# A tile of its own for the unread output of the x3 sums, and four rows of factors in one tile instead of eight in two

## The chip, the cores and the metric

One core of a Trainium2 chip runs the whole program. The time is the device time of one execution in microseconds (us), as the median of three runs. The core has TensorE (PE; PEld are its weight loads), VectorE (DVE), ScalarE (ACT), GpSimd (POOL) and SyncE (SP), which here issues nearly all DMA transfers.

## The reference, cut to what matters

`x` is a field of 256 x 256 tokens with 128 channels. Four layers are added to it one after the other; each reads a group normalisation of `x`. The change lies in the third, which makes x3 out of x2:

```python
zn = _layernorm(z, ln_in_w, ln_in_b)          # z = _gn(x2)
a = sigmoid(zn @ Wga + bga) * (zn @ Wla + bla)
b = sigmoid(zn @ Wgb + bgb) * (zn @ Wlb + blb)
k = jnp.einsum('bimc,bmjc->bijc', a, b)
out = sigmoid(zn @ Wgo + bgo) * (_layernorm(k, ln_o_w, ln_o_b) @ Wlo + blo)
x3 = x2 + out
```

The fourth layer begins with a group normalisation of x3, so the sums of x3 and of its square over all tokens are needed before it can start.

## The kernel before, in words

The channels lie on the 128 partitions, the 65,536 tokens along the free dimension, cut into 32 superchunks of 2048 (`SC`); all data is fp32. The layer has three stages. The first makes `a` and `b` and stores for each token the layer norm's factor, one row of 2048 numbers for each superchunk (`rs2D`). The second, the product stage (L1260 to L1298), multiplies `a` by `b` channel by channel and stores `k`. The third, the x3 stage (from L1305), makes x3 out of x2, `k` and the factors. Within these stages the order of the instructions on each engine is the order in which they are written (`manual_schedule`). Waits follow from the tiles: who writes a tile waits for those who still read or write it.

An iteration `s` of the x3 stage's loop does the following, in two halves `h` of 1024 tokens where a half is named:

- SP: load the row of factors of superchunk s+6 (`load_row7`, L1249), load `k` of s+3 (L1314, four tiles).
- `gate7(s + 3, h)`: TensorE multiplies x2 by the gate's weights (L1334); VectorE adds a column and multiplies by the spread factors into the gate tile (L1344); ScalarE takes the sigmoid in place (L1345). The gate tiles `p7_g` are five, so gate s+5 goes into the tile of gate s. Gates 0 to 2 are made in a prologue ahead of the loop, with the first four spread rows. The gates of superchunks 30 and 31 were made two stages before; iterations 27 to 31 therefore make none.
- TensorE multiplies the normalised `k` of s by the output weights (L1334 again); VectorE adds the bias and multiplies into the gate tile (L1388).
- In half 0, TensorE spreads the layer norm factors of `k` for s+1 over the partitions (L1087), and GpSimd spreads the row of s+4 (`spread_z`, L1328, two tiles). VectorE multiplies `k` of s+1 by its factors (L1323), in each half.
- After both halves, GpSimd adds the gate tile to x2 (L1401), which makes x3 of s. Then `finish7(s - 1)`: ScalarE takes the sum of x3 (L1348) and of its square (L1349) of the superchunk before, through the accumulator of an ACTIVATE whose elementwise output nobody reads; SP stores x3 (L1354). Last SP loads x2 of s+5 (L1258, seven tiles), which needs the tile of s-2: stored and summed.

Each of the ACTIVATEs in L1348 and L1349 must write its output somewhere. Before the change it is the gate tile of the superchunk (`gts.pop(s)` as `junk`).

The rows of factors lie in two tiles, `rs2_0` and `rs2_1`, on the partitions 0, 32, 64 and 96 of each, eight rows in all (`row7`). Six rows are loaded at the head of the product stage (L1279 to L1280), each further one in the loop.

Of the kernel before, what the change touches and what calls it, by code (L numbers as in the profile page):

```python
# [9 lines left out]
F32 = mybir.dt.float32  # L10
# [6 lines left out]
P = 128  # L17
# [3 lines left out]
SC = 2048  # L21
# [11 lines left out]
def kernel(ctx: ExitStack, tc: tile.TileContext, a: dict, out: bass.AP):  # L33
# [205 lines left out]
    with tc.tile_pool(name="x0", bufs=1) as xres, tc.tile_pool(name="p0", bufs=3) as sb:  # L239
        held = {s: xres.tile([P, SC], F32, name=f"x0_{s}") for s in range(RES, NSC)}  # L240
        with tc.tile_pool(name="p0ps", bufs=3, space=PSUM) as ps, tc.tile_pool(
            name="f0ps", bufs=2, space=PSUM
# [167 lines left out]
        with tc.tile_pool(name="p1", bufs=2) as wk_sb, tc.tile_pool(  # L410
            name="p1ps", bufs=4, space=PSUM
# [70 lines left out]
    with tc.tile_pool(name="p2e", bufs=6) as eb, tc.tile_pool(name="p2c", bufs=1) as cs:  # L482
        triT = cs.tile([P, NH, 2, N], F32, name="triT")
        with tc.tile_pool(name="p2", bufs=2) as sb, tc.tile_pool(
            name="p2S", bufs=2, space=PSUM
        ) as psS, tc.tile_pool(name="p2z", bufs=1, space=PSUM) as psZ, tc.tile_pool(
            name="p2M", bufs=3, space=PSUM
# [361 lines left out]
    with x1_scope:  # L849
        with tc.tile_pool(name="p3", bufs=3) as sb, tc.tile_pool(  # L850
            name="p3ps", bufs=3, space=PSUM
# [41 lines left out]
        with tc.tile_pool(name="z", bufs=2) as sb, tc.tile_pool(  # L893
            name="zps", bufs=3, space=PSUM
# [28 lines left out]
            at = turn_z(0)  # L923
            for k in range(16):
                nxt = turn_z(k + 1)
                pz = tri_multiply(nc, ps, at, AB[k // 2][1], k % 2).rearrange("p t n -> p (t n)")
                at = nxt
# [32 lines left out]
        with tc.tile_pool(name="p4", bufs=3) as sb, tc.tile_pool(  # L960
            name="p4psg", bufs=2, space=PSUM
        ) as psg, tc.tile_pool(name="p4psz", bufs=2, space=PSUM) as psz, tc.manual_schedule():
            zs, gts, sums = {}, {}, []
            junk = sb.tile([P, SC], F32, name="p4_junk", bufs=1)
# [41 lines left out]
            for i, s in enumerate(order):  # L1006
# [14 lines left out]
                for h in range(2):  # L1021
                    hs = slice(h * 2 * CK, (h + 1) * 2 * CK)
# [5 lines left out]
                if i in by_dve:  # L1028
                    for h in range(2):
                        hs = slice(h * 2 * CK, (h + 1) * 2 * CK)  # L1030
# [70 lines left out]
    with tc.tile_pool(name="x5", bufs=7) as x5_pool, tc.tile_pool(name="p5", bufs=2) as sb, tc.tile_pool(  # L1101
        name="p5q", bufs=4
    ) as sq_pool, tc.tile_pool(name="p5psX", bufs=1, space=PSUM) as psX, tc.tile_pool(
        name="p5psM", bufs=3, space=PSUM
# [83 lines left out]
        for h, rb in enumerate(broadcast_rows(psM, var, 0, "p5_pm", tag="p5_pm")):  # L1188
            hs = slice(h * H2, (h + 1) * H2)
# [48 lines left out]
    rk_pool = rs2_scope.enter_context(tc.tile_pool(name="rk", bufs=1))  # L1238
    x7_pool = rs2_scope.enter_context(tc.tile_pool(name="x7", bufs=3))
    rk = rk_pool.tile([P, CK], F32, name="rk")  # L1240
    rs2 = [rk_pool.tile([P, SC], F32, name=f"rs2_{i}") for i in range(2)]

    def row7(s):
        at = 32 * (s % 4)
        return rs2[s // 4 % 2][at : at + 1, :]

    def load_row7(s):
        if s < NSC - 2:
            nc.sync.dma_start(row7(s), rs2D[:, s * SC : (s + 1) * SC])  # L1249
# [10 lines left out]
    with tc.tile_pool(name="p6", bufs=3) as sb, tc.tile_pool(name="p6ps", bufs=3, space=PSUM) as ps:  # L1260
        nc.vector.memset(k1, 0.0)
        nc.gpsimd.memset(k2, 0.0)  # L1262
        with tc.manual_schedule():
            quads = {}

            def load6(q):
                if q < D // 4:
                    A = sb.tile([P, 4, 2 * N], F32, name="p6_A")
                    nc.sync.dma_start(A, aD[:, 4 * q : 4 * q + 4, :])
                    B = sb.tile([P, 4, 2 * N], F32, name="p6_B")  # L1270
                    nc.sync.dma_start(B, bD[:, 4 * q : 4 * q + 4, :])
                    quads[q] = A, B

            def turn6(c):
                return tri_turn(nc, ps, sb, quads[c // 4][0], c % 4, ident, nc.vector.tensor_copy)

            for q in range(3):
                load6(q)
            for s in range(6):  # L1279
                load_row7(s)  # L1280
            at = turn6(0)
            for c in range(D):
                q = c // 4
                if c % 4 == 0:
                    K = sb.tile([P, 4, 2 * N], F32, name="p6_K")
                nxt = turn6(c + 1) if c + 1 < D else None
                pz = tri_multiply(nc, ps, at, quads[q][1], c % 4).rearrange("p t n -> p (t n)")
                at = nxt
                nc.scalar.copy(K[:, c % 4, :], pz)  # L1289
                sq = sb.tile([P, 2 * N], F32, name="p6_sq")  # L1290
                nc.scalar.activation(sq, pz, AF.Square)  # L1291
                nc.vector.tensor_tensor(k1, pz, k1, ALU.add)  # L1292
                nc.gpsimd.tensor_tensor(k2, k2, sq, ALU.add)  # L1293
                if c % 4 == 3:
                    nc.sync.dma_start(kD[4 * q : 4 * q + 4, :].rearrange("c (p t) -> p c t", p=P), K)
                    del quads[q]
                    load6(q + 3)
                    if q >= D // 4 - 3:  # L1298
                        load7x(q - (D // 4 - 3), x7_pool, 3)
# [5 lines left out]
    with tc.tile_pool(name="p7", bufs=2) as sb, tc.tile_pool(name="p7psX", bufs=2, space=PSUM) as psX, tc.tile_pool(  # L1305
        name="p7psM", bufs=2, space=PSUM
    ) as psM, tc.manual_schedule():
        ks, rks, rbs, gts = {}, {}, {}, dict(gates)
        AHEAD = 3

        def load7k(s):
            if s < NSC:
                ks[s] = sb.tile([P, SC], F32, name="p7_k", bufs=4)
                nc.sync.dma_start(ks[s], kD[:, s * SC : (s + 1) * SC])  # L1314

        def spread_k(s):
            if s < NSC:
                rks[s] = broadcast_rows(psX, rk, s, "p7_rk")

        def normalise_k(s, h):  # L1320
            if s < NSC:
                hs = slice(h * H2, (h + 1) * H2)
                nc.vector.tensor_tensor(ks[s][:, hs], rks[s][h], ks[s][:, hs], ALU.mult)  # L1323

        def spread_z(s):
            if s < NSC and s not in gates:
                rbs[s] = sb.tile([P, SC], F32, name="p7_rb")
                nc.gpsimd.partition_broadcast(rbs[s], row7(s))  # L1328

        def product7(src, w, h):  # L1330
            pm = psM.tile([P, 2, CK], F32, name="p7_pm")
            for c in range(2):
                k = 2 * h + c
                nc.tensor.matmul(pm[:, c, :], lhsT=w, rhs=src[:, k * CK : (k + 1) * CK], start=True, stop=True)  # L1334
            return pm.rearrange("p c t -> p (c t)")

        def gate7(s, h):
            if s < NSC and s not in gates:
                hs = slice(h * H2, (h + 1) * H2)
                if h == 0:  # L1340
                    gts[s] = sb.tile([P, SC], F32, name="p7_g", bufs=5)
                pg = product7(xs7[s], wf2[:, 4, :], h)
                zg = gts[s][:, hs]
                nc.vector.scalar_tensor_tensor(zg, pg, gcol, rbs[s][:, hs], ALU.add, ALU.mult)  # L1344
                nc.scalar.activation(zg, zg, AF.Sigmoid, bias=b2w[:, 4:5])  # L1345

        def sums7(x, junk, i):
            nc.scalar.activation(junk, x, AF.Identity, bias=m2neg, accum_out=g1[:, i : i + 1])  # L1348
            nc.scalar.activation(junk, x, AF.Square, bias=m2neg, accum_out=g2[:, i : i + 1])  # L1349

        def finish7(s):
            x = xs7.pop(s)
            sums7(x, gts.pop(s), s)
            nc.sync.dma_start(x3T[:, s * SC : (s + 1) * SC], x)  # L1354

        load7k(0)
        load7x(3, sb, 4)
        spread_z(0)
        spread_z(1)

        nc.vector.scalar_tensor_tensor(k1, k1, -1.0 / D, k1, ALU.mult, ALU.mult)
        nc.vector.tensor_tensor(k2, k2, k1, ALU.add)
        nc.vector.tensor_scalar(k2, k2, 0.0, None, ALU.max)
        nc.scalar.activation(k2, k2, AF.Sqrt, bias=epst, scale=1.0 / D)
        nc.vector.reciprocal(k1, k2)
        nc.sync.dma_start(rkD.rearrange("o (p t) -> p (o t)", p=P), k1)
        for c in range(4):
            nc.sync.dma_start(rk[32 * c : 32 * c + 32, :], rkD.rearrange("o (s c t) -> c (o s) t", c=4, t=CK)[c])
        for s in range(1, 3):
            load7k(s)  # L1370
        load7x(4, sb, 4)
        for s in range(3):
            gate7(s, 0)
            gate7(s, 1)
            if s < 2:
                spread_z(s + 2)
        spread_k(0)
        normalise_k(0, 0)
        normalise_k(0, 1)
        for s in range(NSC):  # L1380
            load_row7(s + 6)
            load7k(s + 3)
            last = s == NSC - 1
            for h in range(2):
                hs = slice(h * H2, (h + 1) * H2)
                gate7(s + AHEAD, h)
                pl = product7(ks[s], w2[:, 5, :], h)
                nc.vector.scalar_tensor_tensor(gts[s][:, hs], pl, b2w[:, 5:6], gts[s][:, hs], ALU.add, ALU.mult)  # L1388
                if h == 0:
                    spread_k(s + 1)  # L1390
                    spread_z(s + AHEAD + 1)
                normalise_k(s + 1, h)
                if last:
                    nc.vector.tensor_tensor(xs7[s][:, hs], xs7[s][:, hs], gts[s][:, hs], ALU.add)
                    if h == 0:
                        finish7(s - 1)
                    sums7(xs7[s][:, hs], gts[s][:, hs], s + h)
                    nc.sync.dma_start(x3T[:, s * SC + h * H2 : s * SC + (h + 1) * H2], xs7[s][:, hs])
            del ks[s]
            if not last:  # L1400
                nc.gpsimd.tensor_tensor(xs7[s], xs7[s], gts[s], ALU.add)  # L1401
                if s:
                    finish7(s - 1)
            load7x(s + 5, *((x7_pool, 3) if (s + 5) % 7 < 3 else (sb, 4)))
# [486 lines left out]
```

## Time and profile before

| | us |
|---|---|
| median of 3 runs | 3400.09 |
| lowest, highest | 3397.42, 3402.27 |
| the profiled execution | 3407.79 |
| its span, first to last instruction | 3405.9 |
| TensorE busy | 3094.3 |
| VectorE, ScalarE, GpSimd busy | 2269.6, 2021.2, 1659.1 |
| x3 stage, about | 2648 to 2970 of the span |

A profile line of a group reads: line, engine, operation, output<-inputs, sizes, count, then busy time and mean duration, then the idle time of the engine just before these instructions and who ended it. A wait reads: the waiting engine and line, "<-", the one whose semaphore came last, us in total, times, longest. A line of the timeline or of the chain begins with the start and the duration in us. Idle time of an engine that isn't the bottleneck costs nothing.

### The profile page before, as it was taken

What the parts mean: (1) busy time and instruction counts of PE and PEld (TensorE: products, weight loads), DVE (VectorE), ACT (ScalarE), POOL (GpSimd) and SP (SyncE); (2) the same over time, 40 slices, a digit from 0 to 9 for tenths busy, and PEclk for the clock granted to TensorE, in tenths of its full rate; (3) what the DMA queues carried; (4) which work ended last, traced back from release to release, by engine and by line L of the source; (5) the groups of instructions that cost most, each with busy time, mean ns of one, the idle gap of its engine ahead of it and who ended that gap; (6) DMA issues with size and microseconds to landing.
All of it is one profiled execution on the core that took longest, in us unless ns stands there. A gap on an engine that the chain in (4) does not pass through costs nothing. (4 is left out here: it accounts for less than half of the span.)

```text
span 3405.9 us, 52131 instructions
## 1 busy us (share of the span) xinstructions
PE 3094.3 (91%) x20036; PEld 1645.1 (48%) x20036; DVE 2269.6 (67%) x2613; ACT 2021.2 (59%) x2209; POOL 1659.1 (49%) x904
## 2 busy tenths in 40 slices
PE   5669999999999999967996999999999888769998
PEld 5415555555555555524332444445998333224444
DVE  5627888888888888853555454454555777657776
ACT  3567777777777777734685444443444566635565
POOL 4055777777777777711582000002555666524444
PEclk7899999999999999989997999999999999879999
DMA  9982333333333333379597677676998888756764
GB/s 359 363 315 85 108 120 110 116 115 112 119 108 120 107 120 107 108 287 337 211 401 303 228 282 301 224 270 252 355 348 334 317 310 307 268 162 192 207 186 131
DMA packets 297908, 749.48 MB, mean 220 GB/s; under 512 B 74551, under 2 KB 145161, under 8 KB 248473
## 3 DMA queue, kind: packets, MB, share of 16 engines
q1 hardware_dynamic: 289719, 735.49, 60.5%
q0 software_dynamic: 7648, 9.55, 0.8%
q8 instruction: 161, 2.64, 0.3%
q10 hardware_dynamic: 288, 1.05, 0.1%
q14 instruction: 92, 0.75, 0.1%
HBM read 458.34 MB, written 287.64 MB: 219 GB/s over the span
## 5 line engine op out<-in xcount | busy, mean ns | idle before, releaser
L565 DVE TENSOR_TENSOR p_e<-p_S,triT 128x1024 f32<-128x1024 f32 x512 | 609.4, 1212 | 144.4 <-PE p_S L555 144.4
L575 POOL TENSOR_TENSOR p_es<-p_e 128x1024 f32<-128x1024 f32 x256 | 603.1, 2367 | 125.7 <-issue 65.1
L573 ACT ACTIVATE p_e<-p_e,mbT 128x1024 f32<-128x1024 f32 x512 | 552.0, 1138 | 61.4 <-DVE p_e L565 61.3
L1172 PE MATMUL p_pm<-p_zn,wf 128*128 128x512 f32 x1040 | 449.3, 593 | 2.5 <-ACT p_a L1207 1.9
L540 PE MATMUL p_mm<-p_xn,w 128*128 128x512 f32 x768 | 405.2, 611 | 0.3 <-DVE p_v L535 0.3
L1172 PEld LDWEIGHTS p_pm<-p_zn,wf 128*128 128x128 f32 x1040 | 196.6, 190 | 255.3 <-issue 246.5
L555 PE MATMUL p_S<-p_q,p_k 32*128 32x256 f32 x4096 | 295.5, 401 | 3.5 <-DVE p_e L565 3.3
L1585 POOL TENSOR_TENSOR p_q<-p_q,p_pb 128x2024 f32<-128x2024 f32 x32 | 144.1, 4502 | 259.5 <-DVE p_pb L1579 247.0
L555 PEld LDWEIGHTS p_S<-p_q,p_k 32*128 32x128 f32 x4096 | 186.0, 184 | 159.5 <-PE p_mm L531 91.7
L514 POOL TENSOR_TENSOR p_xn<-p_xn,p_rs 128x1024 f32<-128x1024 f32 x63 | 151.3, 2401 | 205.3 <-DMA p_rb<-rzD 131.7
L1849 PE MATMUL tp_z<-p_B,tp_at 128*128 128x256 f32 x1024 | 250.4, 388 | 0.8 <-DMA p_B<-bD 0.5
L588 PE MATMUL p_o<-p_e,p_v 128*32 128x256 f32 x4096 | 248.5, 383 | 0.0
L1262 POOL MEMSET k<- 128x512 f32 x1 | 0.5, 519 | 507.0 <-DVE p_zn L1165 507.0
L1293 POOL TENSOR_TENSOR k<-k,p_sq 128x512 f32<-128x512 f32 x128 | 163.0, 1273 | 159.4 <-ACT p_sq L1291 159.4
L1849 PEld LDWEIGHTS tp_z<-p_B,tp_at 128*128 128x128 f32 x1024 | 185.2, 191 | 22.7 <-DVE tp_at L1840 1.6
L1401 POOL TENSOR_TENSOR p_x<-p_x,p_g 128x2048 f32<-128x2048 f32 x30 | 136.0, 4535 | 97.9 <-ACT p_g L1345 59.2
L540 PEld LDWEIGHTS p_mm<-p_xn,w 128*128 128x128 f32 x768 | 126.0, 190 | 104.5 <-issue 88.5
L588 PEld LDWEIGHTS p_o<-p_e,p_v 128*32 128x32 f32 x4096 | 120.2, 110 | 110.3 <-ACT p_g L546 41.5
L1292 DVE TENSOR_TENSOR k<-tp_z,k 128x512 f32<-128x512 f32 x128 | 88.5, 691 | 127.1 <-ACT p_sq L1291 127.1
L1334 PE MATMUL p_pm<-p_x,wf 128*128 128x512 f32 x240 | 121.7, 634 | 53.7 <-DVE p_g L1344 51.8
L1289 ACT COPY p_K<-tp_z 128x512 f32<-128x512 f32 x128 | 74.9, 585 | 157.9 <-PE tp_z L1849 157.9
L546 ACT ACTIVATE p_g<-p_mm,bgh 128x512 f32<-128x512 f32 x128 | 87.9, 687 | 131.4 <-PE p_mm L540 131.3
(380 smaller groups left out, 5957.1 us busy)
## 6 DMA issues: line engine op xcount, KB each, us to landing
p_x<-x2T SPq DMA_DIRECT2D x60, 1024.0 KB
x<-x1T SPq DMA_DIRECT2D x51, 1024.0 KB
p_x<-in_x_dram SPq DMA_DIRECT2D x32, 1024.0 KB
p_x<-xT SPq DMA_DIRECT2D x64, 512.0 KB
x2T<-x SPq DMA_DIRECT2D x32, 1024.0 KB
aD<-p_a SPq DMA_DIRECT2D x32, 1024.0 KB
bD<-p_b SPq DMA_DIRECT2D x32, 1024.0 KB
p_A<-aD SPq DMA_DIRECT2D x32, 1024.0 KB
```

The source lines that it names most:

```text
L514: nc.gpsimd.tensor_tensor(xn, xn, groups[g]["rs"], ALU.mult)
L540: nc.tensor.matmul(pm, lhsT=w, rhs=t["xn"][:, cs_], start=True, stop=True)
L555: nc.tensor.matmul(Ss[h // 2][:, h % 2, u, :], lhsT=t["k"][hp, r * N + u * P : r * N + (u + 1) * P], rhs=t["q"][hp, r * N : (r + 1) * N], ...
L565: nc.vector.tensor_tensor(e[:, :, 2 * p : 2 * p + 2, :].rearrange("p u h n -> p h u n"), Ss[p], triT[:, 2 * p : 2 * p + 2, :, :], ALU.add,)
L573: nc.scalar.activation(e[:, u, :, :], e[:, u, :, :], AF.Exp, bias=mbT[:, u, i : i + 1])
L575: nc.gpsimd.tensor_tensor(es, e[:, 0, :, :], e[:, 1, :, :], ALU.add)
L588: nc.tensor.matmul(t["o"][hp, r % 2, :], lhsT=t["v"][:, r * 2 + u, hp], rhs=e[:, u, h, :], start=(u == 0), stop=(u == 1),)
L1172: nc.tensor.matmul(pm[:, c, :], lhsT=wf2[:, i, :], rhs=zns[s][:, k * CK : (k + 1) * CK], start=True, stop=True)
L1293: nc.gpsimd.tensor_tensor(k2, k2, sq, ALU.add)
L1401: nc.gpsimd.tensor_tensor(xs7[s], xs7[s], gts[s], ALU.add)
L1585: nc.gpsimd.tensor_tensor(q[:, :, 1 : N - 2], q[:, :, 1 : N - 2], pb[:, :, 0 : N - 3], ALU.add)
L1849: nc.tensor.matmul(pz[:, t, :], lhsT=at[:, u, t * P : (t + 1) * P], rhs=Bc[:, u, :], start=(u == 0), stop=(u == 1))
```

## The change

The sums write their unread output to a new tile `p7_junk`, which is used for all superchunks; the gate tile is dropped from the table when its superchunk's sums are issued. The rows of factors lie in one tile of four rows instead of two tiles, so that row s+4 takes the place of row s. Four rows are loaded at the head of the product stage. Rows 4 and 5 are loaded in the x3 stage ahead of its loop, after the broadcasts of rows 2 and 3 are issued; rows from 6 on are loaded in the loop as before. The memory of the second row tile and of the new tile is the same, 8 KB on each partition. Lines from L1305 on move down by one to three.

```diff
-    rs2 = [rk_pool.tile([P, SC], F32, name=f"rs2_{i}") for i in range(2)]
+    rs2 = rk_pool.tile([P, SC], F32, name="rs2_")
 
     def row7(s):
         at = 32 * (s % 4)
-        return rs2[s // 4 % 2][at : at + 1, :]
+        return rs2[at : at + 1, :]
...
-            for s in range(6):
+            for s in range(4):
                 load_row7(s)
...
         ks, rks, rbs, gts = {}, {}, {}, dict(gates)
+        junk = sb.tile([P, SC], F32, name="p7_junk", bufs=1)
...
         def finish7(s):
             x = xs7.pop(s)
-            sums7(x, gts.pop(s), s)
+            sums7(x, junk, s)
+            del gts[s]
             nc.sync.dma_start(x3T[:, s * SC : (s + 1) * SC], x)
...
             gate7(s, 1)
             if s < 2:
                 spread_z(s + 2)
+                load_row7(s + 4)
...
-                    sums7(xs7[s][:, hs], gts[s][:, hs], s + h)
+                    sums7(xs7[s][:, hs], junk[:, hs], s + h)
```

## The prediction

> **What bounds the kernel now.** The program is a row of stages, so I read the page for where the x3 stage lies (first gate multiplication 2647.97 us, last sums 2970.5 us) and then looked only there. First the waits of that stretch, longest first; columns: who <- for whom: us in total, times, longest.
>
> ```profile
> ACT p_g L1345 <- DVE p_g L1344: 115.7, 59, 3.9
> ...
> DVE p_g L1344 <- ACT p_g L1349: 67.3, 25, 3.0
> POOL p_x L1401 <- ACT p_g L1345: 59.2, 18, 3.4
> PE p_pm L1334 <- DVE p_g L1344: 51.8, 26, 4.0
> ```
>
> The second line is odd: the gate's multiplication (L1344) waits for the square sum (L1349), although it reads nothing of it. It wants the tile: L1349 wrote its unread output into the gate tile that L1344 is to overwrite, five gates later. 25 times: iterations s = 2 to 26, those in which a gate tile is used again. To see whether this wait ends last, the chain of waits over two iterations (start, us, what):
>
> ```profile
> 2777.39 1.20 DVE p_g L1344
> 2778.59 0.03 issue
> 2778.61 1.15 ACT p_g L1345
> 2779.76 2.00 ACT p_g L1348 x2
> 2781.76 0.02 issue
> 2781.78 2.10 ACT p_g L1349 x2
> 2783.89 0.04 DVEq L1344
> 2783.92 0.04 issue
> 2783.97 0.09 DVE p_g L1344
> ...
> 2787.57 1.20 DVE p_g L1344
> ```
>
> From 2777.39 to 2787.57 is one iteration, 10.18 us (DVE's two k steps, 2784.06 to 2787.57, close the ring). The ring holds VectorE and ScalarE and no TensorE, no transfer, no GpSimd. Then what the stage does without it: TensorE in iterations 1 and 2, before the first reuse of a gate tile.
>
> ```profile
> 2672.01 1.14 PE L1087 MATMUL p_rk<-rk,sel 32*128 32x512 f32 x8
> 2673.07 1.98 PE L1334 MATMUL p_pm<-p_x,wf 128*128 128x512 f32 x4
> ...
> 2680.14 1.14 PE L1087 MATMUL p_rk<-rk,sel 32*128 32x512 f32 x8
> 2683.11 1.12 PE L1334 MATMUL p_pm<-p_x,wf 128*128 128x512 f32 x2 [1.83 <-DVE p_g L1344]
> ```
>
> Between the two L1087 rows lies a whole iteration without an idle entry: 8.13 us. The last row is the first of the stalls. Last the stretches (us, busy time of PE, PEld, DVE, ACT, POOL with counts, clock, DMA share, GB/s):
>
> ```profile
> 2700.00:2870.00 170.00, 137.33 (x402) 52.67 (x400) 119.97 (x100) 105.30 (x99) 114.38 (x34) 1.00 0.84 308
> 2050.00:2250.00 200.00, 200.00 (x636) 83.93 (x638) 99.12 (x74) 93.34 (x76) 0.00 (x0) 1.00 0.74 276
> 1700.00:1780.00 80.00, 78.99 (x258) 29.28 (x259) 47.22 (x71) 66.40 (x65) 64.93 (x22) 1.00 1.02 400
> ```
>
> In the stage's middle PE is busy 81%, the transfers 84%, and no engine is full. The other two rows are yardsticks: PE can be full at clock 1.00, and transfers of the same size can run at 400 GB/s.
>
> **What the Trainium skill says.** "Perfetto Trace Analysis", Optimization Strategy: a gap that repeats on the engine that should be full can mean that the next tile can't be had for lack of buffers. The trace agrees: 2.69 us before L1344 in nearly every iteration. "SBUF — State Buffer", Who interferes with whom: a VectorE instruction with at most one SBUF input, outside the two-port modes, doesn't contend with GpSimd. All three VectorE steps here read one operand from PSUM and one tile from SBUF; L1344 takes at most 1286 ns, median 1283, beside a GpSimd that works two thirds of the time, so I keep the durations for a denser stage. "TensorE: Matmul & The Clock Gate", What's actually happening: activity releases the throttle, idleness brings it. The 2050 to 2250 row agrees (full, 1.00). "DMA: Bandwidth & Descriptors", Where 436 GB/s comes from: a ceiling of 435 GB/s; the trace reaches 400.
>
> **The change, part by part.**
>
> *Sums write to a tile of their own.* The same instructions, the same 2.0 us each. The gate tile is now free when the residual add (L1401) has read it. In the order of the changed build, L1344 has lost its ScalarE wait and keeps VectorE, TensorE and GpSimd. What is late next, per iteration, from rows of this profile: PE 8.13 us as measured; VectorE 2x1.28 + 2x1.28 + 2x1.215 = 7.55; GpSimd add 4.53 + broadcast 2.29 = 6.83; ScalarE 2x1.15 + 1.99 + 2.00 + 2x0.19 = 6.67; transfers 3 x 1.0486 MB + 8 KB = 3.154 MB, at 400 GB/s 7.9 us. PE is last, transfers close behind. The waits that remain, set on an 8.13 us clock from iteration 1: the add of iteration 0 frees its gate tile at 2674.7, wanted at 2671.08 + 8.13 = 2679.2 (4.5 us spare). The row broadcast that L1344 also needs ended at 2685.23, wanted at 2671.08 + 16.26 = 2687.3 (2.1 spare). The x load issued at 2683.29 landed 6.9 us later by its semaphore, at 2690.2; PE wants it three iterations after 2668.48, at 2692.9 (2.7 spare). ScalarE's sums then run 2685.7 to 2689.9 and free the x tile whose next load is issued at about 2691.4 (1.5 spare). None takes the ring's place.
>
> Gain: 25 iterations x (10.19 - 8.13) = 51.5 us. Counted on PE: of its 51.8 us for L1344 one wait of 4.0 lies ahead of the loop, which leaves 47.8. Between them I take **50 us**. The gateless iterations 27 to 31 (about 5.6 us each, PE without a gap) are as before.
>
> *One wait moved.* L1388 now names ScalarE (the sigmoid of three iterations before; it used to be implied). That sigmoid is long done; what can cost is a wait instruction, 21 to 50 ns in L1344's row, 60 of them: 1.3 to 3 us on VectorE, hidden in its 8.13 - 7.55 us per iteration; without that cover, 3 us. Behind a late L1388 stand the normalisation and the next gate. L1348 waits for the earlier square sum, since both write the new tile: a sigmoid pair lies between, so nothing; L1349 behind L1348, which already waits so, shows 0.02 us. 30 of those are 0.6 us, off the path.
>
> *Four rows instead of eight.* Rows 4 and 5 are no longer loaded at the head of the product stage (two issues of about 0.8 us on an SP with nothing waiting: nothing gained) but in the x3 prologue, each behind the broadcast that reads the row's old content (the first two ended by 2649.9; SP gets there at 2656.5: no wait). Row 6 waits for the broadcast that ended at 2652.8 (none), row 7 for the one that ended at 2659.6, which SP reaches at 2658.5 or later: it stands 1.1 us at most, and behind it is only a k load that waits for its tile until 2668.67 anyway. The k and x loads ahead of that slip by two issues, at most 1.7 us, against 6 us and more until they are read. From row 8 on the changed order shows no further wait on GpSimd: SP's earlier store already implies it. Row 4 is needed by a broadcast that ran at 2660.7 and may run until 2668.7 before it delays a gate; even behind the 3 MB issued from 2655.1 (at 400 GB/s 7.9 us) it is there by about 2665. Cost 0, with 3 us, once, as the other end.
>
> Sum: -50 us. The profiled execution took 3407.79 us (span 3405.9, 1.9 around it), 0.2% above the median; no part of the edit depends on that, so the same 50 come off the median: 3400.1 - 50 = **3350 us**.
>
> **Rivals.** *Transfers become the bound.* For: 3.154 MB in 8.13 us is 388 GB/s, 97% of what the 1700 to 1780 row shows, from one queue with a store that must wait for the add. Against: iterations at 400 would need only 7.9, and in the window 2680.5 to 2690.7 this stage itself moved 383. At 373 GB/s (window 2664 to 2672.3) 8.46 us, gain 43; at 341 (product stage) 9.25 us, gain 23. Middle: 3367.
> *The wait is replaced, no change.* L1344 still waits for GpSimd. For it to hold 10.19, two iterations' ring of add, broadcast, gate and k steps (0.15 + 4.54 + 0.09 + 2.29 + 0.1 + 7.08 = 14.3 us) would have to reach 20.4; 16.3 are free. 3400.
> *Slower: the TensorE clock.* Once PE is the bound, a fall of its clock is on the path. At 2876.98 the trace has one: four matmul records took 3.64 us instead of 1.98, some 1.7 us lost. 29 such falls eat the gain; from the 30th the kernel is slower; 40 give 3418. Against: falls follow idleness by the cited page, and the full stage at 2050 has none.
>
> **Numbers.** Forecast 0.70 (gain 43 to 56: 3344 to 3357); transfers 0.17; between or beyond these (gain 7 to 23, over 56) 0.06; no change 0.03; slower 0.04. Two in ten left out: low 3342, high 3368, which takes in about half of the transfer case. 0.2% (6.8 us) is about what a measurement of this kernel tells from no change: faster 0.93, same 0.03, slower 0.04.
>
> **What would show it.** Right: L1344's successor no longer waits for the square sum; PE's 51.8 us fall to a few; PE is busy 97% or more in the loop; an iteration takes 8.1 to 8.3 us. The transfer case: PE or VectorE wait for DMA, share near 1.0, iterations above 8.4. The clock case: clock below 0.9 in the stage. Wrong altogether: L1344 waits for GpSimd, or SP stands at a row load in the loop.

## The result, and the profile after

| | before | after |
|---|---|---|
| median of four runs, us | 3401.18 | 3347.49 |
| lowest to highest | 3397.42 to 3402.57 | 3347.04 to 3348.97 |
| span of the profiled execution | 3405.9 | 3345.3 |
| x3 stage, first gate multiplication to last square sum | 322.7 | 267.8 |

The ratio is 0.9845, with a 95% interval of 0.9828 to 0.9862: 53.7 us less by the medians, 47 to 59 us by the interval.

The waits of the stretch from 2637 to 2918 us of the changed kernel (who <- for whom: us in total, times, longest; "..." stands for lines left out). Behind the change L1345 is the gate's multiplication, L1349 and L1350 are the sums, L1391 is the second product step, L1404 the add, L1329 the broadcast.

```profile
...
ACT p_g L1346 <- DVE p_g L1345: 63.0, 34, 3.3
...
POOL p_x L1404 <- DVE p_g L1391: 31.6, 24, 3.5
...
DVE p_g L1345 <- PE p_pm L1335: 13.6, 31, 1.0
...
POOL p_rb L1329 <- DMA rs__17908<-rs2D: 8.8, 1, 8.8
...
PE p_pm L1335 <- DVE p_g L1345: 2.4, 1, 2.4
```

The line "DVE p_g L1344 <- ACT p_g L1349: 67.3" has no successor: the gate's multiplication now waits for nothing but its product. TensorE's 51.8 us of waiting for it are 2.4, and these lie in the prologue.

The chain of waits over two iterations, from one spreading of the factors of `k` (L1087) to the next but one (start, us, what):

```profile
...
2701.88 1.07 PE p_rk L1087 x8
2702.95 7.06 PE p_pm L1335 x16
2710.01 1.07 PE p_rk L1087 x8
2711.08 7.07 PE p_pm L1335 x16
2718.15 1.07 PE p_rk L1087 x8
...
```

Where the ring of VectorE and ScalarE stood there is TensorE alone, 8.13 us from one spreading of factors to the next. The starts of the gate multiplication in half 0 lie 8.13 or 8.14 us apart in 24 of the 25 iterations from 2 to 26 (one 8.49); before, 10.18 or 10.19 in 22 of 25.

The middle of the stage (us, busy time of PE, PEld, DVE, ACT, POOL with counts, clock, DMA share, GB/s):

```profile
2700.00:2860.00 160.00, 159.92 (x474) 62.33 (x474) 141.74 (x119) 123.50 (x119) 135.24 (x40) 1.00 1.00 388
```

TensorE is full, and the transfers' share is 1.00 as well. Which of the two is the limit can't be read from this row; the last three experiments below tell.

### The profile page after: what moved, and what is told of

Same layout as the page of the kernel before. It is cut to its first block, busy times and chain, and to the rows that moved or that the text cites. A ratio compares the mean times of both kernels' runs of the same rounds, so it can differ in the third digit from the quotient of the medians.

```text
span 3345.3 us, 52187 instructions
## 1 busy us (share of the span) xinstructions
PE 3085.4 (92%) x20036; PEld 1642.6 (49%) x20036; DVE 2269.3 (68%) x2613; ACT 2018.3 (60%) x2209; POOL 1659.9 (50%) x904
## 5 line engine op out<-in xcount | busy, mean ns | idle before, releaser
L531 PEld LDWEIGHTS p_mm<-w,p_xn 128*128 128x128 f32 x1024 | 134.4, 192 | 61.1 <-issue 60.4
L544 ACT ACTIVATE p_k<-p_mm,cqkg 128x512 f32<-128x512 f32 x128 | 88.0, 687 | 125.1 <-PE p_mm L540 124.9
```

## The experiments

Each ratio is to the kernel before as measured beside that run: 3396.74 us for the first three experiments, 3397.47 us for the last three; that of the changed kernel stays the one to 3401.18 us.

Theory: all of the gain is the earlier release of the gate tile, and TensorE takes over at 8.13 us. Rivals: the row half of the change has a part in it; a tile of its own makes the sums cheaper; the transfers are the new limit. The other half of the change alone, the new tile beside eight rows, was not tried: the new tile takes the memory of the second row tile.

### The rows alone

```diff
-        junk = sb.tile([P, SC], F32, name="p7_junk", bufs=1)
...
-            sums7(x, junk, s)
-            del gts[s]
+            sums7(x, gts.pop(s), s)
...
-                    sums7(xs7[s][:, hs], junk[:, hs], s + h)
+                    sums7(xs7[s][:, hs], gts[s][:, hs], s + h)
```

> The rows half of the change alone: one tile of four rows, loads of rows 4 and 5 moved into the x3 prologue; the sums write into the gate tile as before. Theory (the gate tile's release is everything): the ring of 10.19 us stays, L1344 waits for the square sum 25 times, about 67 us; time as before, 3401 within 3 us. Rival (the row tile or the moved loads brought part of the 54 us): between 3347 and 3390. Rival (the moved row loads cost something): 3403 to 3406.

Measured: 3399.83 us; ratio to the kernel before 1.0008, interval 0.9999 to 1.0017. In its waits the old line is back:

```profile
DVE p_g L1344 <- ACT p_g L1349: 67.3, 25, 3.0
```

The row tile and the moved loads are worth nothing measurable, and none of the 54 us is theirs. They only make room.

### Six gate tiles instead of a tile for the unread output

In place of the new tile, a sixth gate tile; the rows as in the edit above:

```diff
-                    gts[s] = sb.tile([P, SC], F32, name="p7_g", bufs=5)
+                    gts[s] = sb.tile([P, SC], F32, name="p7_g", bufs=6)
```

> As rows_only, and six gate tiles instead of five; the sums still write into the gate tile. The 8 KB go to a sixth gate instead of the unread output. Theory: only the release counts. The gate multiplication of iteration s now needs the square sum of s-3 instead of s-2, which is a whole iteration older; the ring is gone and the iteration is TensorE's 8.13 us: 3347 within 3 us, PE full in the loop. Rival (a tile of its own is what makes the difference, e.g. cheaper sums): about 3400. Rival (half undone): 3365 to 3385.

Measured: 3349.12 us, ratio 0.9860 (0.9844 to 0.9875), not to be told from the changed kernel's 0.9845 (the intervals overlap). The middle of its stage:

```profile
2700.00:2860.00 160.00, 160.00 (x475) 63.83 (x474) 142.46 (x119) 124.55 (x120) 134.33 (x39) 1.00 1.00 388
```

The same row as after, with the sums writing where they always did. It was the lack of a free gate tile, not the place of the output. The 8 KB could be spent either way.

### Four gate tiles

To the changed kernel: `bufs=5` becomes `bufs=4` in the same line.

> The changed kernel with four gate tiles instead of five; the sums write to their own tile. Theory: the gate multiplication of iteration s needs the residual add of s-1, which starts 0.15 us after the second product step of s-1 and takes 4.56 us. Ring: 0.15 + 4.56 + 0.1 + 6.35 (from the first gate multiplication to the end of the second product step, as before shows it, 2783.97 to 2790.32) = 11.2 us, so 1.0 us an iteration slower than before: 26 iterations x 1.0, about 3427. The wait shows as L1345 for L1404. Rival (the release of the gate tile had slack beyond one iteration; something else in the change set the time): 3347.

Measured: 3448.97 us, ratio 1.0152 (1.0137 to 1.0168). The wait is the expected one, and its count too:

```profile
DVE p_g L1345 <- POOL p_x L1404: 92.5, 26, 3.6
```

But the kernel lost 52 us where the expectation had 26. After the first two iterations that wait, the starts of the gate multiplication in half 0 lie 11.1 us (once 11.4) or 12.8 us apart, in turn but for one place: half of the iterations are the ring that was forecast as 11.2 us, the others have 1.7 us more. TensorE in one of each (start, us, ..., idle time before):

```profile
2745.70 1.98 PE L1335 MATMUL p_pm<-p_x,wf 128*128 128x512 f32 x4 [2.92 <-DVE p_g L1345]
2747.52 1.88 PE L1335 MATMUL p_pm<-p_k,w 128*128 128x512 f32 x4
...
2756.84 2.64 PE L1335 MATMUL p_pm<-p_x,wf 128*128 128x512 f32 x4 [2.86 <-DVE p_g L1345]
2759.28 2.97 PE L1335 MATMUL p_pm<-p_k,w 128*128 128x512 f32 x4
2762.08 1.88 PE L1335 MATMUL p_pm<-p_x,wf 128*128 128x512 f32 x4
```

The same eight records take 3.5 us in one iteration and 5.2 in the next, from the first start to that of the records behind them, and the granted clock from 2680 to 2970 is 0.92 instead of 1.00. In the second of these iterations it is 0.50 from 2758.0 to 2761.4: 3.4 us at half the clock are the 1.7 us. Between 2696 and 2984 there are 12 such falls in 24 iterations. So the release theory holds with its ring, and my 3427 left out that a TensorE idle for 2.9 us in each iteration loses its clock in half of them. That the idleness is what lowers the clock was not tested by itself here; it is what the Trainium skill says in "TensorE: Matmul & The Clock Gate", What's actually happening. The page names an idle window of about 3.4 us; here gaps of 2.9 us were enough. Why it is half of the iterations and not every one stays open.

### Less work for TensorE, fewer transfers, both

To the changed kernel. The first cut spreads the factors of `k` only once, the second loads every other tile of `k` only; the third kernel has both cuts:

```diff
             if s < NSC:
-                rks[s] = broadcast_rows(psX, rk, s, "p7_rk")
+                rks[s] = rks[0] if s else broadcast_rows(psX, rk, s, "p7_rk")
```

```diff
             if s < NSC:
+                if s % 2:
+                    ks[s] = ks[s - 1]
+                    return
                 ks[s] = sb.tile([P, SC], F32, name="p7_k", bufs=4)
```

> The changed kernel, but the factors of k are spread by TensorE once, for superchunk 0, and used for all (31 of the 32 spreadings of eight records, L1087, are left out; the values of k are thereby scaled wrongly). TensorE's work falls from 8.13 to 7.06 us an iteration, nothing else. Theory A (TensorE is the bound, transfers have 0.2 to 0.7 us of slack): the iteration falls to the next limit, 7.9 us if transfers stop at 400 GB/s, 7.55 us if VectorE comes first; iterations 27 to 31 fall from 5.6 to about 5.0: 3325 to 3339. Theory B (transfers already set 8.13 us, their share is 1.00 in the trace of after): only the last iterations gain, 3343 to 3347.

> The changed kernel, but k is loaded for even superchunks only and the odd one after it uses the same tile (16 of 32 k loads are left out; odd superchunks get wrong values). Transfers fall from 3.154 to 2.63 MB an iteration, TensorE keeps 8.13 us. Theory A (TensorE is the bound): 3347 within 3 us, DMA share about 0.85. Theory B (transfers are the bound): faster, down to TensorE's own time, 3335 to 3343.

> Both cuts: one spreading of factors, and k loaded for even superchunks only. With TensorE at 7.06 us and transfers at 6.6 us an iteration VectorE's 7.55 us (or, by its pipelined starts of 1.19 us, 7.2 us) is next: 25 x 0.6 to 0.9 us and 5 x 0.6 in the last iterations less than after, 3322 to 3330. If less_pe already gives this time, transfers were never near a limit; if less_pe gives 3347 and this 3325, TensorE and transfers were both at their limit.

| | median us | ratio to before | stage us | iteration us |
|---|---|---|---|---|
| after | 3347.49 | 0.9845 (0.9828 to 0.9862) | 267.8 | 8.13 |
| less for TensorE | 3331.50 | 0.9788 (0.9762 to 0.9813) | 254.0 | 7.47, later 7.58 to 8.34 |
| fewer transfers | 3341.17 | 0.9824 (0.9803 to 0.9844) | 267.8 | 8.13 |
| both | 3325.88 | 0.9776 (0.9755 to 0.9797) | 248.0 | 7.47, once 7.56 and once 7.71 |

The rows of the middle, in the same order without after:

```profile
2730.00:2860.00 130.00, 118.87 (x269) 47.17 (x269) 119.49 (x100) 105.25 (x101) 114.56 (x34) 1.00 1.01 406
```

```profile
2700.00:2840.00 140.00, 139.92 (x412) 54.46 (x411) 123.87 (x104) 107.97 (x104) 116.75 (x35) 1.00 0.87 327
```

```profile
2700.00:2840.00 140.00, 135.26 (x300) 53.71 (x300) 133.76 (x114) 116.60 (x113) 128.10 (x38) 1.00 0.91 354
```

A sixth of the transfers gone leaves the stage at 267.8 us to the tenth and TensorE full: TensorE is the limit of the changed kernel, not the transfers. The median alone would have misled: 3341.17 us lies in the range of theory B, 6 us below after's, and below that of theory A. But the intervals of the two ratios overlap, and in the profiled execution, which took 3348.91 us, no iteration of the stage is shorter than after's. Whether the 6 us are more than noise, and where they lie, is not shown. With less for TensorE the first eight iterations take 7.47 us; then x2 comes late. TensorE's waits from 2660 to 2880 us of the kernel with less for TensorE begin with

```profile
PE p_pm L1335 <- DMA p_x<-x2T: 12.6, 18, 1.3
```

and from there the stage runs at the transfers' pace: 3.154 MB at 406 GB/s are 7.77 us, and the 18 iterations from 2723 us on took 7.81 on average. So the transfers stand 0.4 us an iteration behind TensorE, close but not in front. With both cut VectorE and the products alternate at 7.47 us, and TensorE waits for a transfer once, for 0.6 us.

## Why the prediction was right, step by step

- **The ring and its end.** The step "25 iterations x (10.19 - 8.13) = 51.5 us" held in both numbers. From the first to the last of the 25 starts it was 257.0 us and is 203.7: 53.3 less. The 1.8 us beyond 51.5 are three iterations of before that had taken 10.54 to 11.69 us, against one of 8.49 after; the largest holds the fall of the clock at 2876.98 (granted clock 0.50 from 2877.0 to 2880.2; rows_only, with the same ring, has no such fall). Ahead of these starts after is 2.6 us shorter, by a prologue that was faster by chance (below), and behind them 1.0 us longer: the iterations without a gate were not quite as before (42.7 us from the last start to the end of the stage, now 43.6). Together these make the 54.9 us of the stage.
- **The 50 that I took.** The count on TensorE (47.8) was the worse of the two ways: idle time read from matmul records was 1.90 us an iteration where the starts differ by 2.06. By the traces the rate of undisturbed iterations was the better measure. The medians can't tell the two apart: they give 53.7 us here and 47.6 with six gate tiles, which end the same wait. That the forecast of 50 lies 3.7 us from the one and 2.4 from the other is within the noise.
- **No other wait takes its place.** L1345 waits for TensorE only. The tightest margin that I had computed, 1.5 us for the x tile, held: TensorE waits for no x tile, and the store and the load behind it keep their pace of 8.1 to 8.2 us.
- **The moved wait.** L1391 shows no wait for the sigmoid. What it costs is not to be seen on the path.
- **The row loads.** No cost is to be seen: TensorE shows no idle entry from 2649.12 us, where its prologue gates begin, through the iterations that use the first rows, and rows_only took as long as before (its interval leaves room for up to 6 us more). The broadcast of row 4 did wait, until 2665.36, near the 2665 of the prediction:

```profile
2654.30 2.30 POOL L1329 PARTITION_BROADCAST p_rb<-rs__17908  x1 [1.59 <-DVE p_g L1345]
2665.36 2.30 POOL L1329 PARTITION_BROADCAST p_rb<-rs__17908  x1 [8.76 <-DMA rs__17908<-rs2D]
```

  It ended at 2667.7, and the gate that reads it began at 2668.35. The cover was thinner than forecast (0.7 us instead of 3 or more), because this execution's loop began 2.7 us earlier: the prologue's sixteen gate records took 7.1 us, where before they had taken 10.0. The granted clock was 0.50 from 2648.3 to 2655.0 in before, and 1.00 from 2649 to 2656 after. That is no effect of the edit: of the seven profiles with one row tile, four have the short prologue and three the long one. So the cover held, but by less than the prediction's account of it. A thing I had not seen is SP's 1.5 us at row 7, for the landing of a k load ("SPq L1249 <- DMA p_k<-kD: 1.5, 1, 1.5"); the prediction had at most 1.1 us there, for a broadcast. SP standing at a row load in the loop was one of its signs of being wrong altogether. Here it came once and cost nothing: behind it stood only the k load named in the prediction, which was issued at 2665.94, 5.5 us after the row.
- **The rivals.** Transfers as the bound: no, by the stage with fewer transfers; they follow at 7.77 us, and the estimate of 7.9 at 400 GB/s was near. No change: no. The clock: 0.98 over the stage. That the spans differ by 60.6 us and the medians by 53.7 is mostly the rest of the program behind this stage, which took 427 to 435 us in the eight profiles and was at its longest in the one of before.

## What to carry to other kernels

When an instruction waits for one whose result it doesn't read, look at what the latter writes: an output that nobody reads still holds its tile, and in a ring of buffers the step that writes it can be the last to free the tile. Price such a wait by the ring's period against the period of iterations in which the buffers are still fresh; here the first two of the loop gave the new time to 0.01 us. Give the unread output a tile of its own or the ring one more tile: here the two were not to be told apart (0.9845 and 0.9860).

## What the runs showed that was not expected

- TensorE's clock and short gaps: idle for 1.9 us in each iteration it kept clock 1.00 but once in 25 (before), and in all 25 of rows_only; idle for 2.9 us in each iteration it lost clock in 12 of 24, 1.7 us each time, and this cost nearly as much as the longer ring itself (four gate tiles).
- Transfers of 1 MB, two loads to one store, on one queue: 388 GB/s at share 1.00 with TensorE never waiting for one (after), 406 GB/s when they were the limit (less for TensorE). Here a share of 1.00 was not yet the limit.
